# The hidden product of the FFNs by Strassen's seven block products, two elements at a time

## The chip, the cores and the metric

The kernel runs on one core of a Trainium2 chip. The metric is the device time of the slowest core (here the only one) in microseconds; a time is the median of several runs. The core has five engines that run their own instruction streams and wait for each other by semaphores: TensorE (PE, matrix products, with a separate row PEld for its weight loads), VectorE (DVE), ScalarE (ACT, which also evaluates exp and gelu by tables), GpSimd (POOL) and SyncE (SP, which here only issues DMAs). Operands lie in the SBUF, with 128 partitions; matrix products go to the PSUM, 128 partitions of eight banks of 512 floats each.

## The reference

The input x has 16 batch elements of 256 tokens and 256 features, in float32. There are two transformer layers with a condition vector and a context per element:

```python
# layer 0: 16 heads of 64, rotary positions
x = attn(adaln(x, cond)) + x             # self attention
x = attn(adaln(x, cond), ln(context)) + x  # cross attention
h = gelu(adaln2(x, cond) @ ff_w1 + ff_b1)  # (256, 256) @ (256, 1024)
x = h @ ff_w2 + ff_b2 + x                  # (256, 1024) @ (1024, 256)
# layer 1: 16 heads of 16, modulation from silu(cond) @ Wmod
x = x + attn(mod1(x)) @ Wos + bos
x = x + cross_attn(mod2(x), context) @ Woc + boc
x = x + gelu(mod3(x) @ W1 + b1) @ W2 + b2
```

The change concerns the FFN of both layers: first product (256 to 1024 features, "hidden" below), gelu, second product (1024 to 256), added to x.

## The kernel before, in words

The work is a list of 96 jobs: six phases (0 and 1: self and cross attention of layer 0; 2: its FFN; 3 and 4: self and cross attention of layer 1; 5: its FFN), each over the 16 elements. An attention job is walked through in two steps, an FFN job in four (s = 0 to 3). One loop over the steps writes out the instructions of every engine in the order in which that engine runs them. There is no scheduler: what the loop emits first for an engine runs first on it, and what waits there holds all that comes later on that engine. SP is such a queue too: a DMA that waits for its data holds those behind it.

x stays in the SBUF, one tile for each element. The eight PSUM banks are addressed by number. In the FFN phases before, `next_bank()` hands them out in turn.

**Matrix products.** `product` (L82) computes one 128 x n result over 128 contracted features as four matmuls of 32 output columns each; the trace shows each as two records. So a product of 256 columns is 8 records.

**Preparing an element's FFN input.** Three jobs ahead, `prepare_moments` takes mean and variance (DVE, L321 to L325, and rstd on POOL, L327). `prepare_norm` normalizes x on DVE to xh (L335), transposes it in blocks of 32 (L345), sends it to DRAM (SP, L350), and adds the bias of the coming second product to x on POOL (`add_bias`, L420). `prepare_fetch` brings it back turned (SP, L360), so that features lie on partitions, and `prepare_input` applies scale and shift into the tile hT, one half of the features on ACT (L393), the other on POOL (L394).

**Hidden product and gelu.** `ffn_hidden(job, u)` runs once for each of the four steps: two chunks of 128 hidden features by two halves of the input features, four products of 256 columns (all tokens of the element), and two gelus on ACT from PSUM (L701). An element thus has 16 such products. The hidden tiles are called g.

**Second product.** The previous element's second product is computed while the current one's hidden product runs. It is already done by seven block products: `fold_inner` makes five sums of blocks of the hidden tiles on DVE (L733, 128x512 each); the sums of the weights are made once for each phase (`fold_weights`, L724); `finish_folded` runs 7 x 4 products of 128 columns in step 2 and then adds the results to x by five DVE instructions (L747 to L754). The element that ends a phase is finished in the next phase: for phase 2 that is element 15, by the plain `finish` (its x update is L772).

**Neighbours.** The last attention element before an FFN phase still needs its sums (`sum_up`, a reciprocal at L609 and a DMA that spreads it), a scaling on POOL (`scale`, L624) and its output product, which run in the first FFN jobs. In layer 1 these are `normalize` (reciprocal L677, spreading shuffle L685, POOL multiply L686) and `finish`. The modulation vectors of layer 1 are computed in the FFN phase of layer 0, under the elements 2, 5 and 8. In the last phase a reduction over all the softmax sums (`look_outside`, `judge`, `count_outside`) decides whether the fast path was allowed.

ACT must load a table when it changes between exp and gelu (ACT_TABLE_LOAD).

Of the kernel before, what the change touches and what calls it, by code (L numbers as in the profile page):

```python
# [16 lines left out]
P = 128  # L17
# [26 lines left out]
def fast(ctx: ExitStack, tc: tile.TileContext, a: dict, out: bass.AP, flag):  # L44
# [5 lines left out]
    NB = a["x"].shape[0]  # L50
    assert NB >= 11

# [17 lines left out]

    turn_of_ffn = [1]

    def next_bank():
        turn_of_ffn[0] = (turn_of_ffn[0] + 1) % 8
        return turn_of_ffn[0]

    def product(out, lhsT, rhs, start, stop):


        for g in range(4):  # L80
            cut = slice(32 * g, 32 * g + 32)
            nc.tensor.matmul(out[cut], lhsT[:, cut], rhs, start=start, stop=stop)  # L82

# [305 lines left out]

    def affine(pt, cw, scale, bias, tag, name, eng=nc.gpsimd):  # L390

        dst = work.tile([cw, 2, N], F32, tag=tag, name=name)
        nc.scalar.activation(dst[:, 0, :], pt[:, 0, :], AF.Identity, bias=bias(0), scale=scale(0))  # L393
        eng.tensor_scalar(dst[:, 1, :], pt[:, 1, :], scale(1), bias(1), ALU.mult, ALU.add)  # L394
        return dst
# [41 lines left out]
    def prepare_input(job):  # L437

        b, key = job["b"], job["key"]
        factor, addend = job["phase"]["mod"]  # L440
        job["hT"] = hT = affine(
            job.pop("hraw"), P,
            lambda c: factor[:, c, b : b + 1], lambda c: addend[:, c, b : b + 1], "hT", f"hT_{key}",
            nc.vector if b == 0 and job["p"] == 0 else nc.gpsimd,
        )
        if not job["cross"]:
            job["kT"] = hT
        elif job["layer"] == 0:
            job["kT"] = affine(
                job.pop("craw"), P,  # L450
                lambda c: column("L0_xcond_ca_lnc_w", c), lambda c: column("L0_xcond_ca_lnc_b", c),
                "cT", f"cT_{key}",
            )
# [191 lines left out]
    def layer1_sums(job, c, e, at):  # L645
# [12 lines left out]
        if c == 0 and e == 0:  # L658
            job["parts"].append(work.tile([P, 4, N], F32, tag="part", name=f"oT_{key}", bufs=4)[:, 0:2, :])
            job["sums"] = work.tile([P, N], F32, tag="inv", name=f"sums_{key}")  # L660
# [26 lines left out]

    def ffn_hidden(job, u):
        w, key = job["phase"]["w"], job["key"]
        ph = bank(next_bank(), 2, N)  # L690
        if u % 2 == 0:
            job["halves"].append(work.tile([P, 4, N], F32, tag="part", name=f"g_{key}_{u}", bufs=4))
        g = job["halves"][-1][:, 2 * (u % 2) : 2 * (u % 2) + 2, :]
        for c in range(2):
            for k in range(KC):
                product(
                    ph[:, c, :], w[f"w1{u // 2}"][:, k, (2 * (u % 2) + c) * P : (2 * (u % 2) + c + 1) * P], job["hT"][:, k, :],
                    k == 0, k == KC - 1,
                )
        for c in range(2):  # L700
            nc.scalar.activation(g[:, c, :], ph[:, c, :], AF.Gelu, bias=column(w["b1"], 2 * u + c))  # L701
        job["parts"].append(g)

# [30 lines left out]

    def finish_folded(job, at):

        x, weights, hidden = xs[job["b"]], job["phase"]["folded"], job.pop("folded")
        hurry = len(at) == 3
        first, second, third = (bank(i, 4, P) for i in (at if hurry else (*at, at[1])))
        places = {5: first[:, 0], 2: first[:, 1], 4: first[:, 2], 3: first[:, 3],  # L740
                  1: third[:, 0], 7: second[:, 1], 6: second[:, 2]}
        for m in (3, 6, 4, 5, 2, 1, 7) if hurry else places:
            for c in range(4):
                product(places[m], hidden[m][:, c, :], weights[m][:, c, :], c == 0, c == 3)
# [7 lines left out]
        )  # L752
        nc.vector.tensor_tensor(outer, third[:, 0:1, :].to_broadcast([P, 2, P]), outer, ALU.add)
        nc.vector.tensor_tensor(outer, second[:, 1:3, :], outer, ALU.add)  # L754
# [21 lines left out]
    def look_outside():  # L776

        worst = const.tile([P, 2], F32, name="worst")
        every = wtile([P, 4 * NB * 16 * N // P], "wv", "every")
        nc.sync.dma_start(out=every, in_=sums_seen.rearrange("(p n) h r q -> p (n h r q)", p=4 * NB)  # L780
                          .rearrange("p (s m) -> (p s) m", s=P // (4 * NB)))
        return worst, every

    def judge(worst, every):
        nc.vector.tensor_reduce(worst[:, 0:1], every, AX.X, ALU.add)
        nc.vector.tensor_reduce(worst[:, 1:2], every, AX.X, ALU.min)
        nc.vector.tensor_scalar(within[:, 0:1], worst[:, 0:1], SUM_HIGH, None, ALU.is_le)
        nc.vector.tensor_scalar(within[:, 1:2], worst[:, 1:2], 1.0 / SUM_HIGH, None, ALU.is_ge)

    def count_outside():  # L790

        pw = bank(next_bank(), 2)[0:1]
        nc.tensor.matmul(pw, ones, within, start=True, stop=True)
# [107 lines left out]
    for i, (j, s) in enumerate(steps):  # L901
# [4 lines left out]

        late = prev if not ffn else jobs[j - 2] if prev["kind"] == "ffn" else None
        if late is not None and (late["kind"] == "ffn" or late["layer"] == 1):
            late = None
        make_mod = None  # L910
        more = job["p"] + 1 < len(phases)
        if s == 1 and job["b"] == (3 if ffn else 1) and more:
            load_phase(job["p"] + 1, "early")
            if job["layer"] == 1:
                for part in ("first", "last"):
                    load_phase(job["p"] + 1, part)
# [7 lines left out]

        if ffn and layer0 and job["b"] in (2, 5, 8):
            at = phases[3 + job["b"] // 3]
            if s == 0:
                at["make_mod"] = at["mod_load"]()
            if s == 3:
                make_mod = at  # L930
        if ffn and layer0 and job["b"] in (3, 6, 9) and s == 3:
            at = phases[2 + job["b"] // 3]
            at["mod"] = at["mod"]()
# [4 lines left out]
        if ffn:  # L938
            ffn_hidden(job, s)
            if s == 1 and prev["kind"] == "attn" and layer0:  # L940
                sum_up(prev, next_bank())
            if s == 2 and prev["kind"] == "attn" and not layer0:
                finish(prev, next_bank())
            if prev["kind"] == "ffn":
                if s == 0:
                    fold_inner(prev, nc.vector, 5, 2, 1, 7, 6)
                if s == 2:
                    finish_folded(prev, (next_bank(), next_bank()))
            then = attention(i + 2, 1)
            if s == 2 and then:  # L950
                stage_a(then[0], 0, next_bank())
            if s == 0 and prev["kind"] == "attn" and prev["layer"] == 1:
                normalize(prev)
            if late is not None and s == 3:
                finish(late, next_bank())
            if s == 2 and then:
                for t in range(NT):
                    layer1_values(then[0], next_bank(), t)
            if make_mod:
                make_mod["mod"] = make_mod["make_mod"](next_bank())  # L960
            if s == 1 and after is not None:
                prepare_fetch(after)
            if s == 1 and third is not None:
                prepare_moments(third)
                prepare_norm(third)
            if s == 1 and prev["kind"] == "attn":
                fold_weights(job["phase"])
            if s == 3 and after is not None:
                prepare_input(after)
            if s == 3 and prev["kind"] == "attn" and layer0:  # L970
                scale(prev)
        elif layer0:
            then = attention(i + 1, 0)
            stage_t(job, 2 * s, 0)
            stage_t(job, 2 * s, 1)
# [20 lines left out]
            if late is not None and s == 1:  # L996
                if then:
                    finish_folded(late, (4, 5))
                else:
                    finish(late, 7)  # L1000
# [10 lines left out]
            else:  # L1011
                prepare_norm(third)
                prepare_context(third)
                prepare_input(after)
                if job["b"] == 0:
                    fold_weights(job["phase"])
        else:
# [16 lines left out]
            else:  # L1034
                prepare_norm(third)
                prepare_input(after)
        scores(i + 1)
        if job["last"] and s == 0 and job["b"] in (2, 6):
            seen_sums = look_outside() if job["b"] == 2 else count_outside()
        if job["last"] and s == 3 and job["b"] == 3:  # L1040
            judge(*seen_sums)
    fold_inner(jobs[-1], nc.vector, 6, 5, 2, 1, 7)
    finish_folded(jobs[-1], (1, 2, 3))

# [614 lines left out]
```

## Time and profile before

| | before |
|---|---|
| median of 3 runs (lowest, highest) | 2198.17 us (2197.56, 2198.8) |
| profiled execution | 2198.01 us |
| its span, first to last instruction | 2196.1 us |
| granted TensorE clock | 1.000 |
| PE busy | 2181.5 us, 99% |
| DVE busy | 1669.3 us, 76% |
| POOL busy | 1072.3 us, 49% |
| ACT busy | 838.2 us, 38% |
| chain that ended last, share of PE | 92% |

How to read the profile: a group of instructions is written as line, engine, operation, output <- inputs, then partitions x elements; after it come the count, busy time, the mean duration of one in ns, and the idle time of the engine just before such instructions with what ended it. The chain is followed back from the last instruction, at each step to what released it. In the timeline each row has start, length, engine and line; in brackets stands how long the engine was idle before it and what it had waited for. A window's row gives the busy time of each engine in that stretch.

### The profile page before, as it was taken

How to read it: one execution, taken by the hardware profiler on the slowest of the kernel's cores; microseconds unless marked ns; L12 is line 12 of the kernel's file. 1: busy time of each engine (PE TensorE's matmuls, PEld its weight loads, DVE VectorE, ACT ScalarE, POOL GpSimd, SP SyncE). 2: the span in 40 equal slices, each digit the busy share in tenths (PEclk: the TensorE clock that was granted, in tenths of full speed). 3: DMA queues.
4: the chain of work that ended last, by engine and by line, in shares of the span. 5: the costliest groups of instructions: out<-in, count | busy, mean ns of one | idle time of the engine just before them, and what ended most of it. 6: DMA issues, size and time to landing. Idle time of an engine off the chain costs nothing.

```text
span 2196.1 us, 110711 instructions
## 1 busy us (share of the span) xinstructions
PE 2181.5 (99%) x50469; PEld 1437.0 (65%) x50469; DVE 1669.3 (76%) x3119; ACT 838.2 (38%) x1306; POOL 1072.3 (49%) x1036
## 2 busy tenths in 40 slices
PE   9999999999999999999999999999999999999998
PEld 5656656656656666666666668787656656557887
DVE  6877777777787999989898876664777777777654
ACT  3323323323323333333333332334666666663222
POOL 3766566566557767676776752221323232222220
PEclk9999999999999999999999999999999999999999
DMA  6210111110132221212212033221222232223221
GB/s 192 49 37 23 27 37 23 28 37 22 31 89 64 71 60 35 59 41 45 56 37 60 23 74 87 52 45 29 62 43 42 52 95 59 62 52 85 61 62 37
DMA packets 307974, 117.77 MB, mean 54 GB/s; under 512 B 244308, under 2 KB 290728, under 8 KB 307368
## 3 DMA queue, kind: packets, MB, share of 16 engines
q1 hardware_dynamic: 307496, 110.61, 21.5%
q8 instruction: 396, 6.49, 1.3%
q14 instruction: 82, 0.67, 0.1%
HBM read 77.14 MB, written 33.29 MB: 50 GB/s over the span
## 4 chain that ended last, share of the span: by engine, by line
PE 92%; DVE 2%; POOL 2%; DMA 1%; issue 1%; SPq 1%; ACT 0%; DVEq 0%; POOLq 0%; ACTq 0%
PE banks L82 60%; PE banks L566 15%; PE banks L635 9%; PE banks L651 5%; PE banks L502 1%; PE banks L469 1%; POOL raw L624 1%; DVE m L523 1%; POOL qk L531 1%; DMA spread<-sums_seen 0%; POOL folded L733 0%; DMA turned<-blocks 0%; SPq L615 0%; DVE both L587 0%; SPq L350 0%
## 5 line engine op out<-in xcount | busy, mean ns | idle before, releaser
L578 ACT ACTIVATE pr<-banks 128x1024 f32<-128x1024 f32 x576 | 487.6, 938 | 414.3 <-PE banks L566 209.5
L531 POOL TENSOR_TENSOR qk<-m,m 128x512 f32<-128x512 f32 x256 | 347.0, 1376 | 292.5 <-DVE m L523 190.7
L523 DVE TENSOR_TENSOR m<-banks,rope 128x512 f32<-128x512 f32 x512 | 324.1, 679 | 87.1 <-POOL qk L531 83.2
L587 DVE TENSOR_TENSOR both<-pr 128x512 f32<-128x512 f32 x256 | 227.9, 903 | 101.4 <-ACT pr L578 101.2
L642 ACT COPY raw<-banks 128x512 f32<-128x512 f32 x128 | 75.0, 587 | 468.5 <-PE banks L635 461.8
L566 PE MATMUL banks<-qk 32*64 32x256 f32 x8192 | 241.3, 378 | 2.9 <-DVE x L750 2.0
L635 PE MATMUL banks<-pr,v 128*32 128x256 f32 x4096 | 233.2, 379 | 0.0
L566 PEld LDWEIGHTS banks<-qk 32*64 32x64 f32 x8192 | 185.4, 131 | 62.9 <-issue 23.0
L701 ACT ACTIVATE g<-banks,cols 128x256 f32<-128x256 f32 x256 | 106.9, 470 | 288.3 <-PE banks L82 274.9
L635 PEld LDWEIGHTS banks<-pr,v 128*32 128x32 f32 x4096 | 133.1, 110 | 88.5 <-ACT pr L578 0.7
L624 POOL TENSOR_TENSOR raw<-raw,spread 128x512 f32<-128x512 f32 x128 | 164.6, 1318 | 25.4 <-DMA spread<-sums_seen 23.2
L82 PE MATMUL banks<-folded_w,folded 128*32 128x128 f32 x5856 | 175.1, 273 | 0.4 <-POOL folded L733 0.3
L82 PEld LDWEIGHTS banks<-folded_w,folded 128*32 128x32 f32 x5856 | 162.5, 110 | 1.5 <-POOL folded L733 1.5
L593 DVE STREAM_TRANSPOSE squares<-both 128x1024 f32<-128x1024 f32 x128 | 159.4, 1246 | 4.4
L600 DVE TENSOR_REDUCE rows<-squares 128x32 f32<-128x1024 f32 x128 | 155.5, 1215 | 2.2
L686 POOL TENSOR_TENSOR oT<-oT,spread 128x256 f32<-128x256 f32 x64 | 45.7, 735 | 209.9 <-DVE spread L685 209.9
L327 POOL TENSOR_TENSOR rstd<-ve,neg_half 128x2 f32<-128x2 f32 x95 | 75.1, 790 | 144.0 <-DVE ve L325 140.7
L651 PE MATMUL banks<-pr,wide_v 128*32 128x256 f32 x2048 | 134.4, 379 | 1.1 <-ACT pr L578 1.1
L82 PE MATMUL banks<-hT,wk_sa 128*32 128x256 f32 x2048 | 134.9, 381 | 0.1
L420 POOL TENSOR_TENSOR x<-x,bo_b 128x256 f32<-128x256 f32 x96 | 73.1, 781 | 126.1 <-DVE xh L335 126.1
L82 PE MATMUL banks<-hT,wq_sa 128*32 128x256 f32 x2048 | 134.0, 379 | 0.0
L82 PE MATMUL banks<-hT,wq_ca 128*32 128x256 f32 x2048 | 133.9, 379 | 0.0
(157 smaller groups left out, 3669.6 us busy)
## 6 DMA issues: line engine op xcount, KB each, us to landing
turned<-blocks SPq DMA_DIRECT2D x380, 64.0 KB
fetched<-turned SPq DMA_DIRECT2D x380, 64.0 KB
spread<-sums_seen SPq DMA_DIRECT2D x128, 128.0 KB
x<-in_x SPq DMA_DIRECT2D x16, 256.0 KB
fetched_c<-turned_c SPq DMA_DIRECT2D x64, 64.0 KB
cT<-in_ctx_turned SPq DMA_DIRECT2D x16, 256.0 KB
out<-x SPq DMA_DIRECT2D x16, 256.0 KB
ctx<-in_ctx SPq DMA_DIRECT2D x16, 192.0 KB
```

Source lines behind the costliest of these rows:

```text
L82: nc.tensor.matmul(out[cut], lhsT[:, cut], rhs, start=start, stop=stop)
L523: nc.vector.tensor_tensor(m, pq, rope[:, s : s + 1, :].to_broadcast([P, 2, N]), ALU.mult)
L531: nc.gpsimd.tensor_tensor(r, x, y, (ALU.subtract, ALU.add)[out])
L566: nc.tensor.matmul(banks[64 * g : 64 * g + 64, at + h, t * N : (t + 1) * N], lhs, rhs, start=(half == 0), stop=(half == 1 or job["layer"] ...
L578: nc.scalar.activation(pr[:, one], sc[:, one], AF.Exp, scale=0.125 if job["layer"] == 0 else 0.25)
L587: nc.vector.tensor_tensor(job["both"][:, 2 * p : 2 * p + 2, :], pr[:, :, 0, :], pr[:, :, 1, :], ALU.add)
L593: nc.vector.transpose(job["squares"].rearrange("p b k -> p (b k)"), job.pop("both").rearrange("p h n -> p (h n)"))
L600: nc.vector.tensor_reduce(job["rows"][:, u, :], job.pop("squares"), AX.X, ALU.add)
L624: nc.gpsimd.tensor_tensor(part, part, spread[:, u : u + 1, :].to_broadcast([P, 2, N]), ALU.mult)
L635: nc.tensor.matmul(o[32 * h : 32 * h + 32, half, :], v[:, t, col : col + 32], prs[h // 2][:, h % 2, t, :], start=(t == 0), stop=(t == NT - 1),
L651: nc.tensor.matmul(o[32 * h : 32 * h + 32], v[:, t, 4 * c + h, 32 * e : 32 * e + 32], prs[h // 2][:, h % 2, t, :], start=(t == 0), stop=(t ...
L701: nc.scalar.activation(g[:, c, :], ph[:, c, :], AF.Gelu, bias=column(w["b1"], 2 * u + c))
```

## The change

Elements are taken in pairs. The inputs hT of both lie side by side in one tile (`pair`), so that a block of 128 tokens of both elements is 256 columns. The hidden product of a pair is an 8-block product (two halves of the hidden features j, two of the input features k, two of the tokens t), with the weights as blocks a[j][k] of 128 x 512 and the inputs as blocks b[k][t] of 128 x 256. It is replaced by seven block products of four products of 256 columns each: `s1` to `s4` are sums of weight blocks (POOL, once for each phase), `t1` to `t4` sums of input blocks (POOL, for each pair). The partial sums stay in two PSUM banks ("main") which four of the blocks are added up in; after each of the first three, ACT copies the banks off to the SBUF, and DVE adds those copies to the results in "other" and "side", and gelu then runs in place in the SBUF.

The steps are numbered q = 0 to 7 over the pair. In order on PE: q 0 main, side, other; q 1 main; q 2 the second product of the first element of the previous pair; q 3 main; q 4 the second product of its second element; q 5 side; q 6 main. The main banks alternate between 2, 3 and 4, 5 from pair to pair; the second products have banks 0 and 1, side has 6 and 7. Of the five folds for a second product DVE makes three and POOL two.

With this the neighbours move: elements 14 and 15 of phase 2, not 15 alone, are finished plainly in phase 3; some of the last pair's gelus run in phase 3; the modulation is made under elements 2, 4 and 6; the next phase's weights are asked for at element 5, not 3; the late output product of the last attention element goes to element 2; the reduction at the end is split in two tiles; the hidden tiles alternate between two pools of buffers. At the end of phase 5 two elements' second products follow the last block.

```diff
-    def product(out, lhsT, rhs, start, stop):
+    def product(out, lhsT, rhs, start, stop, read_between=False):
...
-            nc.tensor.matmul(out[cut], lhsT[:, cut], rhs, start=start, stop=stop)
+            nc.tensor.matmul(out[cut], lhsT[:, cut], rhs, start=start, stop=stop, skip_group_check=read_between)
...
+    def split_weights(ph):
+        w = ph["w"]
+        a = [[w[f"w1{j}"][:, k, :] for k in range(2)] for j in range(2)]
...
+        nc.gpsimd.tensor_tensor(s1, a[1][0], a[1][1], ALU.add)
+        nc.gpsimd.tensor_tensor(s2, s1, a[0][0], ALU.subtract)
+        nc.gpsimd.tensor_tensor(s3, a[0][0], a[1][0], ALU.subtract)
+        nc.gpsimd.tensor_tensor(s4, a[0][1], s2, ALU.subtract)
...
+    def split_input(job, part):
...
+        if part == 0:
+            nc.gpsimd.tensor_tensor(t1, b[0][1], b[0][0], ALU.subtract)
+            nc.gpsimd.tensor_tensor(t2, b[1][1], t1, ALU.subtract)
+        else:
+            nc.gpsimd.tensor_tensor(t[:, 0], b[1][1], b[0][1], ALU.subtract)
+            nc.gpsimd.tensor_tensor(t[:, 1], b[1][0], t2, ALU.subtract)
...
+        def block(at, left, right, start):
+            for i in range(4):
                 product(
...
+                    banks[:, at + i // 2, i % 2 * N : i % 2 * N + N].rearrange("p (e n) -> p e n", e=2),
+                    left[:, i * P : (i + 1) * P], right, start and i % 2 == 0, True, True,
                 )
+        def join(j, t, at, kept):
+            for e, one in enumerate((job, mate)):
+                for half in range(len(kept)):
+                    n = 4 // len(kept)
+                    nc.vector.tensor_tensor(
+                        one["halves"][j][:, n * half : n * half + n, t * P : (t + 1) * P],
+                        parted(at)[:, n * half : n * half + n, e, :], kept[half][:, :, e, :], ALU.add,
+                    )
+        def kept(tag, n):
+            t = work.tile([P, 4, 2, P], F32, tag=tag, name=f"kept_{key}_{n}", bufs=1)
+            nc.scalar.copy(t.rearrange("p i e n -> p i (e n)"), flat(main))
+            return [t]
+        if q == 0:
...
+            block(main, a[0][0], b[0][0], True)
+            first = kept("both", 0)
+            block(side, s1, job["split"][0], True)
+            block(other, a[0][1], b[1][0], True)
+            join(0, 0, other, first)
+            if pending:
+                gelu(pending[0], 0, every_token)
+        elif q == 1:
+            block(main, s2, job["split"][1], False)
+            job["second"] = kept("squares", 1)
+            if pending:
+                gelu(pending[1], 0, every_token)
+        elif q == 3:
+            block(main, s3, job["split"][2], False)
...
+                nc.scalar.copy(
+                    t.rearrange("p i e n -> p i (e n)"), flat(main)[:, 2 * half : 2 * half + 2, :]
+                )
+                third.append(t)
+            join(1, 1, side, third)
+            for one in (job, mate):
+                gelu(one, 1, second_half)
+        elif q == 5:
+            block(side, s4, b[1][1], False)
+            join(0, 1, side, job.pop("second"))
+        elif q == 6:
+            block(main, a[1][1], job["split"][3], False)
+            for e, one in enumerate((job, mate)):
+                if mate is jobs[-1]:
+                    gelu(one, 0, every_token)
+                gelu(one, 1, first_half, parted(main)[:, :, e, :])
...
+            if q in (0, 4) and third is not None:
+                prepare_moments(third)
...
+            ffn_hidden(one, q)
+            if previous:
+                if q in (0, 3):
+                    folding = jobs[one["index"] - (2 if q == 0 else 1)]
+                    fold_inner(folding, nc.vector, 2, 1, 6)
+                    fold_inner(folding, nc.gpsimd, 7, 5)
+                if q in (2, 4):
+                    finish_folded(jobs[one["index"] - (2 if q == 2 else 1)], (0, 1), (4, 3, 2, 5, 1, 6, 7))
...
+            if q in (1, 5) and third is not None:
                 prepare_norm(third)
+            if q in (2, 4) and after is not None:
                 prepare_input(after)
+            if q in (5, 6) and nxt is not None and nxt["kind"] == "ffn":
+                split_input(nxt, q - 5)
...
-    fold_inner(jobs[-1], nc.vector, 6, 5, 2, 1, 7)
-    finish_folded(jobs[-1], (1, 2, 3))
+    for n in (2, 1):
+        fold_inner(jobs[-n], nc.vector, 2, 1, 6, 5, 7)
+        finish_folded(jobs[-n], (2 * n - 4 + 4 * (n == 1), 2 * n - 3 + 4 * (n == 1)), (4, 3, 2, 5, 1, 6, 7))
```

## The prediction

> **What bounds the kernel now.** I read the page's totals first, then the chain of work that ended last, then two stretches of the FFN phases.
>
> ```profile
> PE 2181.5 (99%) x50469; PEld 1437.0 (65%) x50469; DVE 1669.3 (76%) x3119; ACT 838.2 (38%) x1306; POOL 1072.3 (49%) x1036
> ```
>
> TensorE is busy for 99% of the span, so any matmul that is taken out pays and any wait that is put in costs. The chain, in order of time (start, length, line, records):
>
> ```profile
> 1099.52 3.45 PE banks L635 x64
> 1102.98 6.11 PE banks L82 x224
> ...
> 1333.43 39.06 PE banks L82 x1038
> ...
> 1984.86 203.00 PE banks L82 x5491
> ```
>
> Both FFN phases (about 1291 to 1510 and 1979 to 2190 us) are stretches of PE alone. The first two lines are prices: 3.45/64 = 53.9 ns for a record of 256 columns, 6.11/224 = 27.3 ns for one of 128. One element's period in each FFN phase (columns: PE, PEld, DVE, ACT, POOL busy, clock, DMA share, GB/s):
>
> ```profile
> 1388.18:1401.20 13.02, 13.02 (x359) 10.97 (x355) 7.86 (x19) 3.84 (x10) 2.78 (x4) 1.00 0.30 64
> 2002.05:2015.07 13.02, 13.02 (x360) 10.27 (x356) 7.86 (x20) 3.84 (x10) 2.78 (x4) 1.00 0.53 149
> ```
>
> 13.02 = 128 x 53.9 ns (6.90, hidden product) + 224 x 27.3 ns (6.11, second product): no idle time. Hand-overs and intervals come from the timeline of that stretch:
>
> ```profile
> 1393.19 0.74 DVE L335 TENSOR_SCALAR xh<-x,mv,rstd 128x256 f32<-128x256 f32 x2 [0.82 <-POOL rstd L327]
> 1393.68 1.53 POOL L420 TENSOR_TENSOR x<-x,bo_a 128x256 f32<-128x256 f32 x2 [0.53 <-DVE xh L335]
> ...
> 1398.17 0.39 PE L82 MATMUL banks<-hT,w_a 128*32 128x256 f32 x3
> 1398.61 0.42 DVE L753 TENSOR_TENSOR x<-banks,x 128x256 f32<-128x256 f32 x1 [1.14 <-PE banks L82]
> ```
>
> DVE starts 0.44 after PE has gone on to its next work: that is a hand-over from PE. To PE it is 0.05 (POOL ends at 1984.82, PE starts at 1984.86). The two bias additions start 0.49 after xh and take 1.5. And a place where PE waits today:
>
> ```profile
> 1511.01 1.28 ACT L578 ACT_TABLE_LOAD   x1
> 1512.30 3.83 ACT L578 ACTIVATE pr<-banks 128x512 f32<-128x512 f32 x5
> 1512.95 1.93 PE L82 MATMUL banks<-hT,wqkv_b 128*32 128x256 f32 x32 [1.29 <-ACT pr L578]
> ```
>
> **What the Trainium skill says.** "TensorE: Matmul & The Clock Gate", The mechanism: matmuls run in program order and only weight loads are pulled ahead, so a block that waits holds all behind it. The last line above agrees: 1.29 us of idle PE. "PSUM — Partial Sum Buffer", The four PSUM rules: "Hardware allows a synchronised read of a partial sum in the middle of an accumulation group." That is what the change relies on; no run of before shows it. "SBUF — State Buffer", SBUF: two separate sides: VectorE operations with two SBUF inputs and GpSimd exclude each other. The trace agrees: the same 128x512 sum takes 684 ns as a fold and 903 ns where POOL is busy (groups of lines; busy, mean ns, idle before):
>
> ```profile
> L642 ACT COPY raw<-banks 128x512 f32<-128x512 f32 x128 | 75.0, 587 | 468.5 <-PE banks L635 461.8
> L733 DVE TENSOR_TENSOR folded<-g,g 128x512 f32<-128x512 f32 x93 | 58.6, 684 | 37.3 <-ACT g L701 37.3
> L587 DVE TENSOR_TENSOR both<-pr 128x512 f32<-128x512 f32 x256 | 227.9, 903 | 101.4 <-ACT pr L578 101.2
> L420 POOL TENSOR_TENSOR x<-x,bo_b 128x256 f32<-128x256 f32 x96 | 73.1, 781 | 126.1 <-DVE xh L335 126.1
> ```
>
> **Matmuls removed.** A pair's hidden product takes seven blocks for eight. A block is 32 records, 32 x 53.9 ns = 1.725 us. 16 pairs: **-27.6 us**. Counted in the two instruction listings, hidden work falls by 256 issued matmuls of 256 columns, and one more element (14 of phase 2) is finished unfolded: 64 more of those and 112 fewer of 128 columns. That swap is priced at 0.8 in the handover below. A pair then needs 7 x 1.725 + 2 x 6.11 = 24.3 us of PE against 26.04. What I ask next is which new dependences are longer than the PE work between their ends.
>
> **Wait A, third block to pending element b.** After main's third block (start T) ACT copies its two banks; DVE joins four quarters, and only then, in its order, makes fold 2 of pending element b. The second copy starts at T + 1.725 + 0.44 and ends 0.59 later, at 2.76. Three joins are still behind it, each a PSUM read of 128x256: two such in before start 0.34 apart, so the last ends near 3.80. Fold 2 takes 0.68: 4.48, with the hand-over 4.53. PE wants it after the block and two of the seven products: 1.725 + 2 x 0.873 = 3.47. **1.06 us**, for the 14 pairs that have a pending pair (1 to 7 of both phases): **+14.8**. If joins and fold take the 903/684 longer, 1.4 to 1.6; if the joins overlap more, nothing.
>
> **Wait B, fifth step to the next pair's side1.** The join of side2 (two sums of 128x512, 0.63 apart, 1.26) comes 0.44 after the block; behind it DVE normalizes element four ahead (0.49 to the bias), and POOL, in order, does two biases (1.52) before the next pair's t1 (no such row; the bias of the same shape 0.77). 0.45 + 1.26 + 0.49 + 1.52 + 0.77 + 0.05 = 4.54. PE has main4 and the next main1 meanwhile, 3.45: **1.08 us**, 11 hand-overs (six in phase 2, five in phase 5, where the last has no norm): **+11.9**. It is nothing if the bias starts before the join, and 1.8 if DVE and POOL stretch each other by 903/684.
>
> **First pair of each phase.** It has no pending second products, so the seven blocks stand nearly back to back and nothing covers their chains. Phase 2: side1 waits for x's update (0.44 + 0.69), bias (0.49 + 1.52), POOL's half of hT (0.56), t1 (0.77) and 0.05 = 4.5 after main1's start, 2.75 late; main3 follows main2 directly and waits for the copy of 1024 columns, priced by exp of that size (1036 ns) plus 0.45: 1.5; side2 waits for the joins that read its bank: 1.9. The next pair's main1 needs hT of element 3. Its turning store stands on SP's queue behind the sums and spread of attention's last element, so it goes out at about 14.8, and in before a turn takes 9.44 from issue to hT (1981.20 to 1990.64) plus 0.65: 24.9, against PE's 18.2: 6.5. Side1 again 0.6. Together **+13.2**. Phase 5: 2.45 likewise; finish of element 15 waits for its sums' reciprocal (1.71), now behind the first join: 3.05; side2 1.85; hT of element 3 2.5; side1 0.6; less the 0.4 PE waits there before: **+10.1**. Ends: 8 to 30 for both.
>
> **Handover and end.** Gelus of the last pair move into the next phase; table loads grow from 5 to 9 (1.28 each), mostly where ACT is idle. With the unfolded 0.8, about **+3.1** (0 to 5). At the end two second products follow the last block instead of one; their gelus (about 5.3 us on ACT for two elements) hold the first one back: **+2.3** (1 to 4).
>
> **Costed at nothing.** POOL's split of the weights in phase 4 (four of about 1.4 us) lies in POOL's idle time there; at worst 5.6 once. In phase 2 it runs while PE still has attention's sums. The judging reduction, 4.7 us of DVE in the last phase, is issued once, in step 6, with DVE idle later in the pair; at worst 2. The late second product of attention's last element moves from the second FFN element to pair 1: the same matmuls on PE; its four scalings on POOL (1.32 each, 5.3) now stand behind pair 1's input splits and ahead of pair 2's, half a pair later; were they in the way, at most 1.5 once. ACT's load rises by 3.3 us of copies a pair (three of 1024 columns), on an engine with 9 idle us an element. Loading weights earlier, and the two-tile read, move DMAs only in stretches where DMA share is 0.3 to 0.5. The in-place gelus take 128 columns where before took 256; "ScalarE: Activation LUTs", What ACT_TABLE_LOAD costs, gives about 0.29 us apart (estimate); the trace has 0.37 for 256.
>
> **Sum.** -27.6 + 14.8 + 11.9 + 13.2 + 10.1 + 3.1 + 2.3 = +27.8. The profiled execution took 2198.01 (span 2196.1 and 1.9 around it), within 0.2 of the median 2198.17: **2226 us**.
>
> **Rivals.** *Faster:* the two chains are shorter than I add them. Both exceed their cover by about a quarter (4.53 against 3.47, 4.54 against 3.45); if each is no longer than its cover, A and B vanish, the fills shrink with the same chains to about 14, the ends to 5: -27.6 + 19 = -8.6, 2189.5. It turns at fills plus waits of 27.6. For it: DVE is busy only 7.86 of 13.02 us, so nothing queued should hold the joins. Against it: these are latencies, not loads. *About the same:* waits gone but fills as worked out, -27.6 + 23.3 + 5.4 = +1.1, 2199. *Slower still:* DVE and POOL stretch each other. DVE keeps about 15.7 + 3.9 (joins) - 2.5 (folds given to POOL) = 17 us a pair, but POOL goes from 5.6 to 14.4, with four folds (1.44 each in before) and four splits (0.77). With A at 1.5 and B at 1.8, 21 + 20 + 28.7 - 27.6 = +42, 2240, and up to 2260 if folds on POOL come late too. That the change removes no work is excluded by the count of instructions.
>
> **Chances.** As worked out, 2210 to 2240: 0.58. Slower still, 2240 to 2262: 0.17. Faster, 2186 to 2194: 0.14. About the same, 2194 to 2210: 0.11, of which 0.06 within 0.2% (4.4 us, about what measuring this kernel can tell from no change). So faster 0.14, same 0.06, slower 0.80; the range 2190 to 2250 leaves out less than 0.2.
>
> **What would show it.** Hidden records of 1792 a phase against 2048. PE idle about 1.1 us with DVE's fold as its releaser at the third of b's seven products, 14 times; PE idle 1.1 us with POOL's split as releaser at side1, 11 times; a pair's period near 26.4. Two stretches of 10 to 13 idle us at the heads of the FFN phases; nine table loads. I am wrong if a pair's period is 24.3 to 25, if PE's idle time stands elsewhere, or if attention's phases change.

## The result and the profile after

The changed kernel takes 2230.94 us (median of six runs, 2230.67 to 2234.39), the kernel before 2197.88 in the same comparison: 33 us more, a ratio of 1.0156 with a 95% interval of 1.0143 to 1.0169. 2226 had been forecast. First the totals of the page after:

```profile
PE 2172.8 (98%) x49861; PEld 1409.7 (63%) x49861; DVE 1697.4 (76%) x3186; ACT 914.4 (41%) x1502; POOL 1198.1 (54%) x1164
```

There are 608 fewer records on PE, exactly the listing's count (2 x 192 + 2 x 112): the work did go. But its busy time fell by 8.7 us only, while the span rose by 32.4 (2228.5 against 2196.1). A busy PE is not a PE at its full rate: about 6 us of the busy time are stretches at half clock, shown below, and in a pair 0.43 us are the modelled ends of matmuls that nothing follows (24.73 busy for 24.30 of work). Here is one pair of elements in each FFN phase, in the same columns as the two windows of before:

```profile
1424.90:1450.93 26.03, 24.73 (x672) 19.34 (x672) 17.34 (x43) 12.13 (x31) 13.36 (x16) 1.00 0.23 50
2096.27:2122.30 26.03, 24.76 (x674) 19.37 (x674) 18.06 (x46) 12.14 (x32) 13.34 (x16) 1.00 0.27 64
```

A pair takes 26.03 us, within 0.01 us what two elements took before (2 x 13.02), although it has 1.73 us less to multiply. The view of PE's waits (what was waited for: us in total, times, longest) says where PE stood still:

```profile
PE banks L76 <- DVE folded L849: 11.6, 16, 0.7
PE banks L76 <- POOL split L722: 10.6, 13, 2.2
PE banks L76 <- ACT hT L387: 5.3, 1, 5.3
PE banks L76 <- ACT pr L579: 3.2, 4, 1.6
PE banks L76 <- DVE g L769: 3.1, 2, 1.6
PE banks L76 <- DVE ve L319: 2.8, 1, 2.8
PE banks L76 <- POOL oT L687: 2.7, 1, 2.7
PE banks L567 <- DVE wide_v L487: 1.9, 1, 1.9
```

The first row is wait A (14 of the 16; the other two are at the end), the second wait B (11 of 13; the others are the two first pairs' t1). Below them stand the heads of the phases and the handover. The row `DVE ve` (2.8) belongs to wait B's kind too: the weight load of the same block names POOL's split as its releaser, and that t1 ended at 2026.64, just before PE's start. Before, no row was over 2.0 us, and inside the two FFN phases the view shows no wait of PE at all.

Both chains can be followed link by link in one pair. Wait A, the timeline of after (third block from 1446.55):

```profile
1448.58 0.59 ACT L802 COPY kept<-banks 128x512 f32<-128x512 f32 x1 [0.28 <-PE banks L76]
1449.19 1.09 DVE L769 TENSOR_TENSOR g<-banks,kept 128x256 f32<-128x256 f32 x3 [0.44 <-ACT kept L802]
1450.20 1.28 DVE L849 TENSOR_TENSOR folded<-g,g 128x512 f32<-128x512 f32 x2
1450.93 1.30 PE L76 MATMUL banks<-w_a,folded 128*32 128x128 f32 x40 [0.73 <-DVE folded L849]
```

PE's start lies 4.38 after the third block's; without a wait it would have been 3.47: 0.91. The bracket says 0.73 because it counts from the modelled end of the matmul before, which overlaps its successor; from start to start is the honest measure. Wait B in the same pair:

```profile
1431.27 1.29 DVE L769 TENSOR_TENSOR g<-banks,kept 128x512 f32<-128x512 f32 x2 [0.85 <-PE banks L76]
1432.47 0.73 DVE L329 TENSOR_SCALAR xh<-x,mv,rstd 128x256 f32<-128x256 f32 x2
1432.97 1.53 POOL L414 TENSOR_TENSOR x<-x,bo_a 128x256 f32<-128x256 f32 x2 [4.07 <-DVE xh L329]
1434.45 0.72 POOL L722 TENSOR_TENSOR split<-hT 128x256 f32<-128x256 f32 x1
1435.23 1.93 PE L76 MATMUL banks<-split,split_a 128*32 128x256 f32 x32 [0.57 <-POOL split L722]
```

From 1431.02, where PE went on from side's block, to 1435.23 are 4.21 us, of which two blocks cover 3.45: 0.76.

The two stretches at the heads hold something that no step had priced. Windows of after: three blocks that follow a wait, the first also in the timeline.

```profile
1315.93:1319.40 3.47, 3.47 (x36) 1.70 (x40) 0.00 (x0) 2.01 (x8) 3.39 (x5) 0.54 0.70 144
2011.30:2014.58 3.28, 3.19 (x32) 1.34 (x36) 1.51 (x4) 0.00 (x0) 2.65 (x4) 0.62 0.14 26
2026.70:2028.45 1.75, 1.75 (x33) 1.06 (x36) 0.00 (x0) 0.00 (x0) 1.73 (x3) 1.00 0.67 107
```

```profile
1315.93 3.50 PE L76 MATMUL banks<-hT,w_a 128*32 128x256 f32 x32 [5.26 <-ACT hT L387]
```

The block of 32 records takes 3.33 us (1315.93 to the next at 1319.26) and not 1.73: after waiting 5.26 us PE was granted 0.54 of its clock over this window (the number behind POOL's). This happened four times, at 1315.93, 1516.90, 2001.54 and 2011.30, and cost about 6 us. The four waits, 12.0 us in all, were thus paid one and a half times.

### The profile page after: what moved, and what is told of

The parts are those of the page before. It is cut to its first block, busy times and chain, and to the rows that moved or that the text cites. A ratio compares the mean times of both kernels' runs of the same rounds, so it can differ in the third digit from the quotient of the medians.

```text
span 2228.5 us, 109880 instructions
## 1 busy us (share of the span) xinstructions
PE 2172.8 (98%) x49861; PEld 1409.7 (63%) x49861; DVE 1697.4 (76%) x3186; ACT 914.4 (41%) x1502; POOL 1198.1 (54%) x1164
## 4 chain that ended last, share of the span: by engine, by line
PE 90%; DVE 4%; POOL 3%; issue 1%; ACT 1%; DMA 1%; SPq 0%; DVEq 0%; ACTq 0%; POOLq 0%
PE banks L76 57%; PE banks L567 15%; PE banks L636 9%; PE banks L652 5%; PE banks L503 1%; DVE g L769 1%; PE banks L470 1%; POOL x L414 1%; DVE folded L849 1%; POOL raw L625 1%; POOL folded L849 0%; ACT kept L802 0%; POOL split L722 0%; DVE m L524 0%; POOL qk L532 0%
## 5 line engine op out<-in xcount | busy, mean ns | idle before, releaser
L76 PE MATMUL banks<-folded_w,folded 128*32 128x128 f32 x5760 | 168.7, 273 | 0.2 <-POOL folded L849 0.2
L567 PE MATMUL banks<-q,k 32*64 32x256 f32 x4096 | 130.5, 385 | 2.0 <-DVE wide_v L487 1.9
L769 DVE TENSOR_TENSOR g<-banks,kept 128x512 f32<-128x512 f32 (+1 forms) x128 | 65.4, 552 | 85.9 <-PE banks L76 68.1
```

The costliest lines, as they stand in the source:

```text
L567: nc.tensor.matmul(banks[64 * g : 64 * g + 64, at + h, t * N : (t + 1) * N], lhs, rhs, start=(half == 0), stop=(half == 1 or job["layer"] ...
```

## The experiments

All times are medians beside runs of the kernel before on the same chip (2198.1 to 2198.5 in these sets). My theory was that latency chains cause the loss, each fixed by the order in which instructions stand in a queue. The rival was that DVE and POOL together are the bound (17 and 13 us of a 26 us pair, and slower when both run), so that a new order would only move the wait.

**1. Split ahead of the bias**

```diff
+            if q == 5 and nxt is not None and nxt["kind"] == "ffn":
+                split_input(nxt, 0)
             if q in (1, 5) and third is not None:
                 prepare_norm(third)
...
-            if q in (5, 6) and nxt is not None and nxt["kind"] == "ffn":
-                split_input(nxt, q - 5)
+            if q == 6 and nxt is not None and nxt["kind"] == "ffn":
+                split_input(nxt, 1)
```

> Edit: in step 5 of a pair POOL makes the next pair's t1 and t2 before the two bias additions of prepare_norm, not after them. Theory (latency chains A and B): the idle 0.57 us with POOL split L722 as releaser goes from the pairs' first steps; from start to start each costs 0.75, eleven of them, and one longer one at the second pair of phase 5 (2.8) shrinks by the biases' 1.5: 2230.9 - 9.5 = 2221. Wait A stays at 0.7. Rival (DVE and POOL together are the bound, the order only shows where it is felt): the pair's period stays near 26.0 us, the wait shows up at another line, 2228 to 2231.

Measured: 2219.28, ratio to before 1.0099 (1.0083 to 1.0114), 11.7 us less than the change. The eleven waits on POOL's split are gone; the three that are left stand in the first pairs and at the second pair of phase 5:

```profile
PE banks L76 <- POOL split L722: 5.5, 3, 2.2
```

Two us more than expected went with them. In this run's trace the clock fell twice and not four times, which is worth about 3 us, and the wait for hT of element 3 was shorter (4.6 for 5.3).

**2. Folds ahead of the joins**

```diff
+            if previous and q == 3:
+                fold_inner(before, nc.vector, 2, 1, 6)
+                fold_inner(before, nc.gpsimd, 7, 5)
             ffn_hidden(one, q)
             if previous:
-                if q in (0, 3):
-                    folding = jobs[one["index"] - (2 if q == 0 else 1)]
+                if q == 0:
+                    folding = jobs[one["index"] - 2]
```

> Edit: in step 3 the folds of the pending second element are issued before the copies and joins of the third block, not after them. Theory: the idle 0.73 us with DVE folded L849 as releaser goes; from start to start it costs 0.91, fourteen times: 2230.9 - 12.7 = 2218. Wait B stays. Rival (bound by DVE and POOL): the joins now come later and the wait moves to side's next block or the next fold; 2228 to 2231.

Measured: 2216.46, 1.0087 (1.0073 to 1.0100), 14.5 us less, 1.8 more than expected. The wait on DVE's folds fell from 16 times to the two at the end:

```profile
PE banks L76 <- DVE folded L849: 1.4, 2, 0.7
```

**3. Both**

> Both edits. Theory: they add up, a pair's period is its PE work of 24.4 us, 2230.9 - 22 = 2209, still slower than before because of the first pairs, the handover and the end. Rival: one of the two waits comes back at the other place, 2215 to 2228.

Measured: 2207.94, 1.0046 (1.0032 to 1.0059). Alone they gave 11.7 and 14.5, together 23.0: as expected (22), and 3.2 short of their sum; the two falls of the clock in run 1's trace are four again in this one. A window of this kernel over one pair:

```profile
1418.50:1442.80 24.30, 24.30 (x680) 19.54 (x676) 17.73 (x43) 12.34 (x30) 13.40 (x16) 1.00 0.24 48
```

PE is busy for the whole 24.30 us, the 24.3 of the working, while DVE and POOL do the same 17.7 and 13.4 us as in the change. The rival falls for the pairs: there was room on both engines, only the order was wrong. There was room even though a fold of two hidden tiles now takes DVE 959 ns on average. And this kernel is still slower than before, so the rest is in the heads, the handover and the end.

**4. The heads, first attempt**: on top of 3, elements 2 and 3 are normalized in attention's last job, and t1 to t4 of pair 0 come first there.

```diff
+            elif nxt["kind"] == "ffn":
+                prepare_input(after)
+                for part in range(2):
+                    split_input(nxt, part)
+                prepare_norm(third)
+                prepare_moments(jobs[j + 4])
+                prepare_norm(jobs[j + 4])
...
-            if q in (1, 5) and third is not None:
+            if (q == 5 or q == 1 and job["b"]) and third is not None:
```

> Both edits, and for the first pair of each FFN phase: element 3 is normalized and sent to be turned in attention's last step, and t1 to t4 of pair 0 are made ahead of the norm of element 2. Theory: the 5.3 us wait of the second pair's main1 in phase 2 falls to 1 or less, side1 of pair 0 comes 1 to 2 us earlier in both phases, the 2.8 at the second pair of phase 5 goes: some 8 us less than the run with both edits, 2201. Rival: POOL and DVE are full at that place (split of the weights, scaling of attention's last elements), the work that is brought forward delays side1 as much as it saves; 2207 to 2212.

Measured: 2201.60, 1.0016 (1.0008 to 1.0024). 6.3 us for the 8 expected, but not in the way expected. In its timeline (ACT, then PE):

```profile
1308.17 0.60 ACT L387 ACTIVATE hT<-fetched,add_a,fac_a 128x256 f32<-128x256 f32 x1 [6.44 <-DMA fetched<-turned]
```

```profile
1310.57 3.64 PE L76 MATMUL banks<-hT,split_a 128*32 128x256 f32 x32 [6.76 <-DVE g L769]
```

hT of element 2 stands ahead of the third block's copies on ACT. Now element 3's store comes ahead of element 2's fetch on SP, the fetch is late, ACT waits for it, and the copies, the joins and side's next block wait behind ACT. The 5.3 us had moved, not gone; what this run gained stands mostly in the row of POOL's split, which went from 5.5 us to 1.1.

**5. The heads, second attempt**: element 2 normalized a step earlier in attention's last job, element 3 ahead of attention's last sums, the sums' reciprocal ahead of the first join, element 2 fetched in attention.

```diff
                 if nxt["kind"] == "ffn":
+                    prepare_norm(third)
+                    prepare_moments(jobs[j + 4])
...
+            if s == 1 and nxt["kind"] == "ffn":
+                prepare_turn(jobs[j + 4])
...
+            if q == 0 and early and before["layer"] == 1:
+                normalize(before)
             ffn_hidden(one, q)
```

> Both reorderings of the pairs, and for the first pair of each FFN phase: elements 2 and 3 are normalized and sent to be turned within attention's last job, element 2 is fetched there, t1 to t4 of pair 0 are made ahead of the last bias, and in layer 1 the reciprocal of element 15's sums stands ahead of the first join. Against the run with both reorderings alone (2207.9). Theory (the heads are chains that start too late): the waits of 5.1 (hT of element 3), two of 2.2 (t1), 2.7 (oT) and 1 of the second pair in phase 5 go; 1.5 (side's bank) in both phases and 1.2 (copy before main3) stay because they lie between blocks; 2195, below the kernel before. Rival (DMA queue: every turn takes the same time on SP's queue and stands behind the sums' spread, so bringing it forward only moves the wait, as it did in the last run, where 5.2 us came back at the third copy): 2200 to 2204.

Measured: 2203.46, 1.0024 (1.0016 to 1.0031): the rival's number. What is brought forward now stands in front of attention's own work on DVE. Its timeline, PE at the heads of phases 2 and 5:

```profile
1300.31 1.93 PE L76 MATMUL banks<-split,split_a 128*32 128x256 f32 x16 [2.57 <-DVE x L890]
...
1991.02 3.50 PE L76 MATMUL banks<-split,split_b 128*32 128x256 f32 x32 [2.62 <-DVE sums L674]
```

PE waits for two PSUM banks that DVE has not yet read, while the waits for hT and for attention's oT are gone.

**6. Handover and end alone**, on top of 3: layer 1's `wide_v` tiles out of the buffers that the pairs' inputs use, an exp of one column after the moved gelus, and the last folds ahead of the last x updates.

```diff
-            wide_v.append(work.tile([P, NT, 8, 64], F32, tag="v", name=f"wide_v{i}"))
+            wide_v.append([work.tile([P, 8, 64], F32, tag="folded", name=f"wide_v{i}_{t}", bufs=5) for t in range(NT)])
...
+                gelu(jobs[j - 1 - s], 0, every_token)
+                fetch_exp()
...
     for n in (2, 1):
         fold_inner(jobs[-n], nc.vector, 2, 1, 6, 5, 7)
-        finish_folded(jobs[-n], ...)
+    finish_folded(jobs[-2], (0, 1), (4, 3, 2, 1, 6, 5, 7))
+    finish_folded(jobs[-1], (2, 3), (4, 3, 2, 5, 1, 6, 7))
```

> Both reorderings of the pairs, and only the handover to phase 3 and the end changed: layer 1's wide_v tiles no longer share buffers with the pairs' inputs, the exp table is loaded right after the moved gelus by an exp of one column, and at the end the folds of both last elements come ahead of the x updates, product 1 and 6 ahead of 5 in the first. Theory: 1.9 (wide_v) + 1.2 (table) + 0 to 1.3 (first table) + 1.8 (two waits of 0.9 at the end) go: 2207.9 - 6 = 2202. Rival (the gelus themselves and not table or buffers hold the exp of phase 3): 2205 to 2207.

Measured: 2202.44, 1.0022 (1.0015 to 1.0029): as expected, but not by the buffers. The wait on `wide_v` is still there:

```profile
PE banks L568 <- DVE wide_v L488: 1.6, 1, 1.6
```

The fill stands behind hT of the next phase on POOL, and that hT waits for PE's last block. What went are the table's 1.2, the two waits at the end and, in this trace, the half clock that followed the wait on `wide_v`. So part of the agreement with the forecast is luck.

**7. All of it**

> All of it: pairs, heads, handover and end. Theory: the seven blocks save 27.6 in full and about 8 to 10 us of waits are left in heads and handover; 2189, 0.3 to 0.5% below the kernel before. Rival (the waits are tied to each other and come back elsewhere): 2196 to 2202, no better than before.

Measured: 2199.48, 1.0005 (0.9997 to 1.0013), no different from before. With the heads of run 5 the theory's number was not reached.

**8. The heads, third attempt** (its expectation calls it the second), on top of 3: as in 4, but element 2's hT after the copies; in phase 5 element 2's norm a step earlier, and element 3's behind attention's last sums and the reciprocal, ahead of the first join.

```diff
+            if q == 0 and early and before["layer"] == 1:
+                normalize(before)
+                prepare_norm(third)
             ffn_hidden(one, q)
...
-            if q in (2, 4) and after is not None:
+            if q == 4 and nxt is not None and jobs[one["index"] - 1]["kind"] == "attn":
+                prepare_input(nxt)
+            if (q == 4 or q == 2 and previous) and after is not None:
                 prepare_input(after)
```

> Both reorderings of the pairs and a second attempt at the heads. In phase 2 the work of attention's last job stands as in the first attempt (input sums, then the norms of 2 and 3), but element 2's scale and shift come after the third block's copies on ACT, so that their wait for the DMA holds nothing. In phase 5 element 2 is normalized a step earlier, and the sums' reciprocal and element 3's norm stand ahead of the first join but behind attention's last sums. Theory: what came back in the two earlier attempts was the order in a queue (ACT waiting for a DMA ahead of the copies, 5.2; DVE normalizing ahead of sums that hold side's bank, 2.6; DVE's backlog in phase 1, 4.9), not work; of the waits of 16 us in both heads about 6 stay (copy 1.2, side's bank 1.5 twice, about 1 for t1 and 1 for hT): 2207.9 - 10 = 2198. Rival (DMA and DVE are full there): 2201 to 2204 as before.

Measured: 2195.17, 0.9984 (0.9978 to 0.9991), 12.8 us below run 3 and 3 us below the forecast: faster than before for the first time. So in the heads, too, it was the order. But the waits alone do not make 12.8: those of the heads fell from 17.6 us in run 3 to 9.6. The rest is the clock. Run 3's trace has four stretches at half clock, run 5's has three, and this one has none before the last matmul; the last section shows what sets them off.

**9. The same heads with handover and end**, and the `wide_v` fill ahead of the next hT on POOL.

```diff
+            if q == 4 and attention(i + 4, 1) and not wide_v:
+                zero_values()
```

> The same heads with the changed handover and end, and layer 1's wide_v tiles filled before the next phase's hT on POOL's queue. Theory: 2199.5 (all of it, first attempt) - 3.7 (head of phase 2) - 2.8 (head of phase 5) - 1.7 (wide_v): 2191 to 2193, 0.2 to 0.3% below the kernel before. Rival: the head's waits come back, 2197 to 2200.

Measured: 2190.99 (2190.10 to 2191.92), 0.9965 (0.9952 to 0.9979): 0.35% below the kernel before, at the lower edge of the 2191 to 2193 that the theory gave. The row of `wide_v`'s first wait is gone, so it was the order on POOL; 1.2 us of it came back as a wait for ACT's moved gelus. What PE still waits for, the first rows:

```profile
PE banks L76 <- ACT hT L388: 4.0, 2, 2.6
PE banks L76 <- DVE g L779: 3.1, 2, 1.5
PE banks L76 <- ACT pr L583: 2.5, 2, 1.7
```

**10. A control**: the kernel before with the exp of one column after its FFN phase's last gelu.

```diff
+        if u == 3 and job["b"] == NB - 1 and job["p"] == 2:
+            one = stat.tile([P, 1], F32, tag="fetch_exp", name="fetch_exp")
+            nc.scalar.activation(one, mask[:, 0:1], AF.Exp)
```

> A control: the kernel before, with one thing of the best version that is not of the change, the exp of one column right after the FFN phase's last gelu, so that the table load does not wait for the first scores of layer 1. If this is worth what the trace shows there (table load 1.28 us in a wait of 1.29), 2198.1 - 0.6 to 1.3 = 2197; then at most 1.3 of the 7 us that the best version gains are owed to it. If the order alone made the best version faster, this one would come near it, 2191 to 2194.

Measured: 2197.94, 1.0000 (0.9991 to 1.0008): nothing that can be measured; an effect of 1.3 us would lie within the interval. The trace says why:

```profile
1515.31 1.93 PE L82 MATMUL banks<-hT,wqkv_b 128*32 128x256 f32 x32 [1.39 <-ACT pr L578]
```

The wait of 1.29 us is still there: gelu, table load and hT follow each other on ACT without a gap, so the load comes earlier but the exp does not. Whether other reorderings would help the kernel before was not tried. In its FFN phases there is nothing for them to remove, as the view shows no wait of PE there.

## Why the prediction was right, step by step

The path was right: PE bound, seven blocks for eight saved, and the saving lost to two dependences between neighbouring pairs and to uncovered chains at the heads. The nine table loads are there too (five before). That the total came within 5 us is in part luck: the two waits were forecast 5.7 too long, the heads and the handover 7.4 too short. The sizes, forecast against measured (from start to start in the timeline of after):

| step | forecast | measured | how measured |
|---|---|---|---|
| matmuls | -27.6 | -27.6 | 608 fewer records; a pair's PE work of 24.30 in run 3 |
| wait A, 14 pairs | +14.8 | +12.7 | 0.91 each |
| wait B, 11 hand-overs | +11.9 | +8.3 | 0.75 each |
| head of phase 2 | +13.2 | +12.9 | first block to pair 1's late product 32.0, less 11 blocks and the sums |
| head of phase 5 | +10.1 | +13.4 | pair 0's start to pair 1's first second product 34.5, less 11 blocks and finish, less 0.4 |
| handover, with the swap | +3.1 | +7.5 | phases 3 and 4 are 13.6 longer, of which 6.9 moved matmuls; the swap 0.8 |
| end | +2.3 | +2.1 | last block to the end 21.0 against 12.9, less 6.1 |

With 0.85 for the judging reduction (costed at nothing; the pair that has it takes 26.88) and 0.8 that phases 0 and 1 took longer, this makes 30.9 of the span's 32.4; 1.5 stay unassigned.

A and B are smaller mainly because I took 0.44 or 0.45 for the hand-over from PE: here DVE starts 0.25 after PE goes on (1431.02 to 1431.27) and ACT 0.31 (the second block of wait A starts at 1448.27, the copy at 1448.58). That is 0.13 of A's 0.15 and 0.20 of B's 0.33; every other link was within 0.1 of the forecast.

In the heads the sums hide errors that cancel. In phase 2 PE's idle time was 11.2 us, 2 less than forecast: hT of element 3 cost 5.4 for 6.5 (whose own working, 24.9 against 18.2, gives 6.7), and the second side1 nothing for 0.6. The clock's drop, which no step had, brought 1.6 back. In phase 5 the idle time was about 10, as forecast, but not where it was forecast: hT of element 3 was in time (0 for 2.5), and the second side1 cost 3.0 for 0.6, because POOL made the two biases ahead of t1 as in wait B, and DVE was late with the norm. The drops of the clock made it 13.4.

The handover was the mis-sized term, and lies outside its range of 0 to 5. The fill of layer 1's `wide_v` tiles stands behind the next hT on POOL, and that hT waits for the last block; the first scores of layer 1 therefore wait 1.9 us and run at half clock afterwards, which cost about 1.6. The fill also shares the buffers of tag `v` with the pair's input tile, which I took for the cause at first; run 6 shows that they are worth 0.3 us at most, and run 9 that it was the order. Two exps behind the moved gelus took 1.7 and 1.2 more than in the same places before, and a later wait on `wide_v` 0.6.

On the rivals: *faster* and *about the same* are out, since both waits are there in nearly every pair, 14 and 11 times. *Slower still* is out for a pair, because run 3 hides both chains without less work on DVE or POOL. Folds on DVE did stretch: the prediction compared two different instructions for this (684 and 903 ns), but the same fold of two hidden tiles took 684 ns on average before, 791 in the change and 959 in run 3. There two of them take 1.28 us at 1433.82, with POOL idle, and 2.05 at 1441.18, beside POOL's own fold. That is off the path once the order is right.

The points from the Trainium skill: "TensorE: Matmul & The Clock Gate", The mechanism, was borne out, each late operand held every matmul behind it (5.26 us at 1315.93). The partial sum's read between blocks, on which "PSUM — Partial Sum Buffer", The four PSUM rules, was quoted, stands in the trace as stated; the copy took 1013 ns for 1024 columns, against the 1036 that were assumed.

## What to carry to other kernels

Taking work from the busiest engine only pays as far as the new dependences are shorter than the work that lies between their ends; add up each new chain, hand-overs included, against that cover. Here each missed by 0.75 to 0.9 us, and moving the folds and the split elsewhere in the order hid both, with the same work. When a step is brought forward, look at what it then stands in front of on every queue, the DMA queue and ACT's wait for it included: the three attempts on the heads differ mainly in that, and lie up to 8 us apart, a part of it through the clock.

## What was not expected of the hardware

After some waits PE was granted only half its clock: 3.41 us at 0.50, which cost 1.4 to 1.7 us each. The length of the wait alone does not decide it: after 1.9, 2.2, 2.7 and 5.3 us idle it happened, after 2.2 (1296.92) and 2.8 (2026.70) it did not; and the same wait of 2.62 us for attention's sums is followed by a block of 3.50 us in run 5 and of 1.93 in run 7.

What decides is where the wait lies. In the clock records of each of the twelve traces all changes lie multiples of 3.413 us apart. Cut into stretches on this grid, the two runs differ. Run 5, then run 7:

```profile
1987.43:1990.84 3.41, 0.97 (x20) 0.31 (x12) 2.53 (x7) 1.01 (x1) 3.06 (x5) 1.00 0.48 77
1990.84:1994.25 3.41, 3.23 (x32) 1.80 (x36) 3.37 (x7) 0.00 (x0) 2.39 (x4) 0.50 0.48 76
```

```profile
1984.57:1987.98 3.41, 2.63 (x52) 1.30 (x40) 2.49 (x10) 0.71 (x1) 2.82 (x5) 1.00 0.27 45
1987.98:1991.39 3.41, 1.56 (x32) 1.15 (x36) 3.41 (x8) 0.30 (x1) 3.33 (x6) 1.00 0.40 65
1991.39:1994.80 3.41, 3.41 (x69) 2.48 (x65) 3.31 (x7) 0.00 (x0) 2.08 (x3) 1.00 0.53 112
```

In run 5 PE is idle for 2.44 us of one stretch, and the next is granted 0.50. In run 7 an edge of the grid divides the wait into 0.78 and 1.84 us, and nothing happens. The change, before and after the wait on `wide_v` and then at the wait of 2.8 us:

```profile
1513.72:1517.13 3.41, 1.55 (x26) 0.59 (x26) 1.03 (x3) 2.59 (x9) 2.35 (x3) 1.00 0.00 0
1517.13:1520.54 3.41, 3.35 (x62) 1.94 (x48) 2.24 (x6) 1.80 (x3) 1.50 (x2) 0.50 0.02 5
2022.30:2025.71 3.41, 1.59 (x32) 0.68 (x24) 3.38 (x12) 3.34 (x10) 2.52 (x4) 1.00 0.00 0
2025.71:2029.12 3.41, 2.42 (x48) 1.48 (x52) 0.93 (x4) 0.91 (x3) 3.33 (x6) 1.00 0.48 76
```

Over the twelve traces, their first 25 us left out, each of the 27 stretches with 2.2 us or more of idle PE was followed by one at 0.50. With up to 1.84 us none was, unless it was at half clock itself (one case, run 4, 1.70 us). Between 1.85 and 2.01 us both occurred (1.86 led to it, 2.01 did not). This is read from the traces of kernels made for other questions; nothing was varied to test it. The grid lies differently in each execution, so how often a wait near 2 to 3 us costs the clock is partly chance.

The Trainium skill, "TensorE: Matmul & The Clock Gate", Part 1, describes such a gate with a window of about 3.4 us that runs freely of the kernel. The grid agrees with that. The page gives a whole idle window as the condition, while here some 1.9 to 2.2 us of one sufficed; the measured numbers decide.
